# Column sums from strips: another form for the bias shifts, key sums and end terms of a four-layer network kernel

## The chip, the cores and the metric

The kernel runs on one core of a Trainium2 chip. The metric is the device time of one execution in microseconds (us). One launch computes the whole network for two images, one after the other on the same core.

## The reference

The input is two images of 512 channels and 64 x 64 pixels. Four layers follow each other, each in the form "x plus a branch of the group-normalised x" (32 groups of 16 channels):

```python
x = x + _L0_conv_ref(_gn(x), ...)   # window attention and pooled tokens
x = x + _L1_conv_ref(_gn(x), ...)   # deformable attention
x = x + _L2_conv_ref(_gn(x), ...)   # mixture of max pools
x = x + _L3_conv_ref(_gn(x), ...)   # random-feature ("favor") attention

def _gn(v, G=32, eps=1e-5):
    g = v.reshape(B_, G, C_ // G, H_, W_)
    m = jnp.mean(g, axis=(2, 3, 4), keepdims=True)
    s = jnp.var(g, axis=(2, 3, 4), keepdims=True)
    return ((g - m) / jnp.sqrt(s + eps)).reshape(v.shape)
```

The kernel never writes the normalised image. A projection `W.T @ (x - m) / s` is computed as `(W / s).T @ x` plus a bias per output channel, `(W / s).T @ (-m)`: a product of a 512 x 512 matrix with one vector, called the bias shift below. It is needed for W_sr, W_q and both halves of W_kv in layer 0, for w_q in layer 1, and for Wq, Wk and Wv in layer 3.

Layer 3 also needs sums over all 4096 tokens:

```python
qp = _favor_softmax_features(q, proj, is_query=True)
kp = _favor_softmax_features(k, proj, is_query=False)   # ratio * (exp(..) + EPS)
context = jnp.einsum('bhnm,bhnd->bhmd', kp, v)
k_sum = jnp.sum(kp, axis=-2)
denom = jnp.einsum('bhnm,bhm->bhn', qp, k_sum)
out = jnp.einsum('bhnm,bhmd->bhnd', qp, context) / denom[..., None]
```

`k_sum` is 256 feature sums for each of 8 heads. The constant EPS in the query's features makes two further terms, called end terms below: EPS times the sum of `context` over the 256 features (64 values a head), and EPS times the sum of `k_sum` (one value a head).

## The kernel before

An image lies in SBUF as X, 128 partitions by four chunks of channels (KC = 4) by 4096 pixels, in fp32. Y, of the same size, is scratch and later takes the next image. Work is done in blocks of 512 pixels (TB, one PSUM bank), eight blocks an image (NB). Almost all products run in fp32; in the profile each fp32 matmul shows as two MATMUL records with a LDWEIGHTS each.

The program is written down per engine as a chain of Python generators that are advanced in turn (`in_turn`), and a scheduler then fixes one order of instructions for each engine, adds the waits and hands out the buffers. An engine runs its instructions in that order, so an instruction that waits holds up all behind it on its engine.

The places that matter here, for each of the two images:

- **Layer 0, `pooled_tokens` (L1844).** W_sr is scaled by rows with 1/s on VectorE (`scale_rows`, L103), its bias shift is made (`shift_bias`, L108, called at L1851), and then 8 blocks of 4 projections run (`project`, L131, matmuls at L134), each read out by a Gelu on ScalarE (L1857) and two sums on VectorE. After blocks 1, 2 and 3 the weights of q, k and v are scaled and their shifts made (L1869).
- **Layer 1 (L984).** One shift, for `bq`. The next products (L1046) and the Gelu behind them need it.
- **Layer 3, `key_context` (L1365).** A shift for `bk` (L1375), and two rows: `v_row` (L1377), the shift of V as a row spread over all partitions, and `vmean` (L1410), the mean of V. Both come from `shift_row` (L122): four accumulating matmuls of 128x512 with the vector as the stationary operand, spread to 128 columns. Then keys and values of block n+1 are prepared (`prepare`) while block n is contracted (`contract`); POOL adds the exponentials of every head into `asum` (L1436). While the last block is contracted, the first query block is prepared: `Queries.first` makes the shift `bq3` (L1541).
- **Layer 3, `contexts` (L1456).** Once all keys are done: the largest score of each head (L1461 to L1472, `lost`), its product with the mean of V (`lv`, L1475), then for both halves j of the 256 features four transposes of the accumulated context (L1481) and sixteen one-column products that sum `asum` (L1489), and last thirty-two one-column products for the end terms (L1501). The queries' scores (L1693) follow on TensorE.

`shift_bias` is sixteen matmuls: for each of four output chunks, four accumulating products of a 128x128 block of the weights (stationary) with one column of `nmean` (moving). `contexts` uses the same form: a block of data is loaded as stationary operand and a single column of ones is moved through it. All of these write a few columns of one PSUM bank, which VectorE then reads (L118, L120, L1491, L1503).

All the pools of PSUM together hold 8 banks. In layer 0 the ring of working banks has 5, in layer 3's key part it has 8.

Of the kernel before, what the change touches and what calls it, by code (L numbers as in the profile page):

```python
# [33 lines left out]
    C_SD) = (0, 128, 256, 384, 512, 514, 540, 572, 573, 589, 717, 765, 797, 863)  # L34
C_N = 927
# [898 lines left out]
class Net(General):  # L934
# [14 lines left out]

    def local_bound(self, sp_scale, wp, pp):  # L950
# [14 lines left out]
    def layer1(self, X, Y, d):  # L965

        tc, nc, vec = self.tc, self.nc, self.vec
        with tc.tile_pool(name="l1", bufs=1) as sp:
# [5 lines left out]
            with tc.tile_pool(name="l1a", bufs=1) as wp, \  # L974
# [9 lines left out]
                self.shift_bias(bq, wq, nmean, pp)  # L984
# [380 lines left out]
    def key_context(self, X, Y, d, nmean, rstd, mv, queries, kp, wp, pp):  # L1365
# [9 lines left out]
        self.shift_bias(bk, wk, nmean, pp)  # L1375
        row = kp.tile([P, C], F32, name="v_row")
        self.shift_row(row, wv, nmean, pp)  # L1377
# [7 lines left out]
        def prepare(blk):  # L1385
# [70 lines left out]
    def contexts(self, top, acc, asum, vmean, queries, kp, pp):  # L1456
# [20 lines left out]
        yield  # L1477
        for j in range(2):
# [6 lines left out]
            ps = pp.tile([P, TB], F32, name="mm")  # L1485
            for h in range(NH):
                for i in range(2):
                    lo = i * NK + j * P
                    nc.tensor.matmul(ps[:, h:h + 1], asum[h][:, lo:lo + P], self.one[:, :1],  # L1489
                                     start=(i == 0), stop=(i == 1))  # L1490
            nc.vector.tensor_tensor(ksum[:, j, :], ps[:, :NH], lost, ALU.add)  # L1491
            yield
        ends = queries.ends
        ps = pp.tile([P, TB], F32, name="mm")
        for i in range(2):
            for g in range(NH):
                ch = slice(g % 2 * HD, (g % 2 + 1) * HD)
                for j in range(2):
                    src = ksum[:, j, g:g + 1].to_broadcast([P, HD]) if i else ctxm[:, j, g, :]
                    at = i * KC + g // 2  # L1500
                    nc.tensor.matmul(ps[ch, at:at + 1], src, self.one[:, :1], start=(j == 0),  # L1501
                                     stop=(j == 1))
        nc.vector.tensor_scalar(ends, ps[:, :2 * KC].rearrange("p (i c) -> p i c", i=2), 1e-4,  # L1503
                                None, ALU.mult)
# [19 lines left out]
class Queries:  # L1524
# [197 lines left out]
class Local:  # L1722
# [121 lines left out]
    def pooled_tokens(self):  # L1844
# [6 lines left out]
        net.shift_bias(bias, w, self.nmean, self.pp, self.vec[:, V_BSR:V_BSR + KC])  # L1851
        for blk in range(NB):
# [11 lines left out]
            if 1 <= blk <= 3:  # L1864
# [4 lines left out]
                net.shift_bias(self.bias["qkv"[i]], w3, self.nmean, self.pp,  # L1869
# [619 lines left out]
```

## Time and profile before

| | us |
|---|---|
| median of 3 runs | 5323.94 |
| lowest and highest of these | 5315.73, 5334.31 |
| the profiled execution's own time | 5318.67 |
| its span, first to last instruction | 5316.9 |
| TensorE busy in it | 4985.0 |
| VectorE, ScalarE, POOL busy | 3203.0, 1807.7, 1800.7 |
| mean granted TensorE clock | 0.965 |

The groups that the change touches, summed from the trace of this execution for both images: the one-column matmuls of `shift_bias` (L115) are 448 records, those of the key sums (L1489) 128, those of the end terms (L1501) 128; the matmuls of `shift_row` (L127) are 32.

How to read it: TensorE is busy for 94% of the span, but matmuls are pipelined and the record of one is longer than the time by which it delays the next. So the durations of single records are not added up below; the distance from the first record of a stretch to the start of what follows it is used. "Granted clock" is the share of the full TensorE clock that the chip's throttle allowed in a stretch.

### The profile page before, as it was taken

What the parts mean: (1) busy time and instruction counts of PE and PEld (TensorE: products, weight loads), DVE (VectorE), ACT (ScalarE), POOL (GpSimd) and SP (SyncE); (2) the same over time, 40 slices, a digit from 0 to 9 for tenths busy, and PEclk for the clock granted to TensorE, in tenths of its full rate; (3) what the DMA queues carried; (4) which work ended last, traced back from release to release, by engine and by line L of the source; (5) the groups of instructions that cost most, each with busy time, mean ns of one, the idle gap of its engine ahead of it and who ended that gap; (6) DMA issues with size and microseconds to landing.
All of it is one profiled execution on the core that took longest, in us unless ns stands there. A gap on an engine that the chain in (4) does not pass through costs nothing. (4 is left out here: it accounts for less than half of the span.)

```text
span 5316.9 us, 48977 instructions
## 1 busy us (share of the span) xinstructions
PE 4985.0 (94%) x17531; PEld 2129.3 (40%) x17531; DVE 3203.0 (60%) x3944; ACT 1807.7 (34%) x3441; POOL 1800.7 (34%) x1196
## 2 busy tenths in 40 slices
PE   7999999899988899999999999998999888999998
PEld 4423333554333344533344333335543334445333
DVE  4267777645679733477732677766456796333766
ACT  1245665234222233222112556652432122333221
POOL 0035565401310045444500355553013100454544
PEclk9999999999989999999999999999999899999999
DMA  3035556500000000211210355564000000000111
GB/s 145 2 79 139 145 141 172 151 18 24 1 1 0 1 1 1 64 43 52 73 55 2 91 141 143 141 176 135 18 24 1 1 0 1 1 1 17 40 46 43
DMA packets 124753, 309.89 MB, mean 58 GB/s; under 512 B 20882, under 2 KB 33682, under 8 KB 122964
## 3 DMA queue, kind: packets, MB, share of 16 engines
q1 hardware_dynamic: 124500, 306.67, 21.0%
q8 instruction: 141, 2.31, 0.2%
q14 instruction: 112, 0.92, 0.1%
HBM read 258.10 MB, written 48.50 MB: 58 GB/s over the span
## 5 line engine op out<-in xcount | busy, mean ns | idle before, releaser
L134 PE MATMUL mm<-big,w 128*128 128x512 f32 x2560 | 1191.2, 610 | 9.8 <-DVE late L2252 9.8
L134 PEld LDWEIGHTS mm<-big,w 128*128 128x128 f32 x2560 | 468.8, 192 | 693.6 <-issue 577.2
L2298 POOL TENSOR_TENSOR late<-late,big 128x1024 f32<-128x1024 f32 x192 | 454.1, 2365 | 204.0 <-DVE big L2293 188.5
L1266 POOL TENSOR_TENSOR total<-prob 128x512 f32<-128x512 f32 x128 | 159.6, 1269 | 758.6 <-ACT prob L1263 758.6
L1183 PE MATMUL acc<-big,dg 128*128 128x512 f32 x704 | 320.0, 613 | 55.6 <-DVE big L698 25.4
L1436 POOL TENSOR_TENSOR big<-big 128x512 f32<-128x512 f32 x224 | 277.5, 1270 | 222.8 <-ACT big L1427 222.8
L2220 POOL TENSOR_TENSOR late<-late 128x512 f32<-128x512 f32 x128 | 160.8, 1276 | 521.3 <-ACT late L2209 499.5
L2293 DVE TENSOR_TENSOR big<-big,mm 128x512 f32<-128x512 f32 x384 | 255.3, 681 | 122.8 <-ACT mm L2285 109.0
L698 DVE TENSOR_TENSOR big<-big 128x3968 f32<-128x3968 f32 x72 | 308.8, 4289 | 6.2
L2285 ACT COPY mm<-big 128x512 f32<-128x512 f32 x428 | 244.4, 593 | 196.0 <-DMA big<-rows 162.8
L1427 ACT ACTIVATE big<-mm,ed 128x256 f32<-128x256 f32 x512 | 193.8, 488 | 259.3 <-DVE top L1423 227.0
L1283 DVE RECIPROCAL recip<-psD 128x512 f32<-128x512 f32 x64 | 214.9, 3357 | 87.2 <-PE psD L1280 87.2
L2298 POOL TENSOR_TENSOR late<-late,tap 128x1024 f32<-128x1024 f32 x96 | 227.2, 2366 | 103.3 <-DVE tap L2293 100.1
L1263 ACT ACTIVATE prob<-mm 128x512 f32<-128x512 f32 x256 | 132.0, 605 | 364.4 <-PE mm L1260 359.2
L1423 DVE TENSOR_REDUCE top<-mm 128x1 f32<-128x512 f32 x256 | 159.1, 683 | 148.2 <-PE mm L1361 147.9
L1678 PE MATMUL mm<-k,w 128*128 128x512 f32 x512 | 236.3, 606 | 9.9 <-DVE k L1671 6.5
L2160 DVE TENSOR_TENSOR prod<-qs,big 128x1024 f32<-128x1024 f32 x192 | 230.3, 1215 | 8.3 <-PE tap L2173 6.3
L1401 PE MATMUL mm<-w,big 128*128 128x512 f32 x512 | 234.5, 601 | 0.0
L134 PE MATMUL mm<-big,big 128*128 128x512 f32 x512 | 232.6, 615 | 0.0
L1183 PEld LDWEIGHTS acc<-big,dg 128*128 128x128 f32 x704 | 136.3, 196 | 236.8 <-issue 193.5
L134 PE MATMUL mm<-big,wq 128*128 128x512 f32 x512 | 230.6, 599 | 0.0
L548 PE MATMUL mm<-big,wo 128*128 128x512 f32 x512 | 224.5, 596 | 0.0
(375 smaller groups left out, 8152.3 us busy)
## 6 DMA issues: line engine op xcount, KB each, us to landing
big<-rows SPq DMA_DIRECT2D x428, 256.0 KB, 4.3
tap<-rows SPq DMA_DIRECT2D x212, 256.0 KB, 4.3
yd<-late SPq DMA_DIRECT2D x32, 512.0 KB, 3.0
lost_all<-lost SPq DMA_DIRECT2D x128, 128.0 KB, 3.1
out<-big SPq DMA_DIRECT2D x64, 256.0 KB, 2.0
big<-in_W_kv SPq DMA_DIRECT2D x8, 1024.0 KB, 6.2
rows<-late SPq DMA_DIRECT2D x64, 128.0 KB, 2.4
big<-yd SPq DMA_DIRECT2D x16, 512.0 KB, 5.1
```

The source lines that it names most:

```text
L134: self.nc.tensor.matmul(ps, w[:, kc, :], X[:, kc, blk * TB:(blk + 1) * TB], start=(kc == 0), stop=(kc == KC - 1))
L548: nc.tensor.matmul(ps, w[:, kc, oc * P:(oc + 1) * P], att[:, kc, :], start=(kc == 0), stop=(kc == KC - 1))
L698: nc.vector.tensor_tensor(o, a, b, ALU.max)
L1183: nc.tensor.matmul(accs[b], dg, src[:, b * TB:(b + 1) * TB], start=(j == 0), stop=(j == 6))
L1283: nc.vector.reciprocal(r, psD)
L1401: nc.tensor.matmul(ps, X[:, kc, lo:lo + P], wv[:, kc, :], start=(kc == 0), stop=(kc == KC - 1))
L1436: nc.gpsimd.tensor_tensor(a, a, part, ALU.add)
L1678: nc.tensor.matmul(ps, self.wo[:, kc, oc * P:(oc + 1) * P], qs[:, kc, :], start=(kc == 0), stop=(kc == KC - 1))
L2160: self.nc.vector.tensor_tensor(self.prods[k % 3].rearrange("p (y x) -> p y x", x=W), qs, self.kx[:, y + dy:y + dy + self.UY, dx:dx + W], A ...
L2285: nc.scalar.copy(ps, part)
L2293: nc.vector.tensor_tensor(part.rearrange("p (y x) -> p y x", x=W), self.vx[:, y:y + self.UY // 2, dx:dx + W], ps.rearrange("p (y x) -> p y ...
L2298: nc.gpsimd.tensor_tensor(out, out, t, ALU.add)
```

## The change

Three pieces of arithmetic are written in another form; the sums are the same.

- `shift_bias` becomes `shift_columns`. Four matmuls of 32x512 (`shift_strips`) take one chunk of `nmean`, spread to 32 columns, as stationary operand and move the 512 weights of the chunk through it. Chunk kc writes partitions 32 kc to 32 kc + 31 of one bank. ScalarE copies the bank to a scratch tile in SBUF. Four matmuls then take 128 columns of that tile as stationary operand and one column of a constant (`C_ROW`, which has a one in one row of each strip) as moving operand, which adds the four strips and turns the row to a column. VectorE writes the result as before.
- `shift_row` becomes `shift_rows`: the strips, the copy, and then one matmul of 128x512 in place of the four accumulating ones.
- In `contexts` the key sums are made as strips: eight matmuls of 32x512 whose stationary operand is a constant of ones in every other column (`C_EVEN`), two for each of four strips. ScalarE copies one half of the bank, VectorE adds the other half, two transposes turn the strips to columns, and VectorE adds `lost`. The end terms come from VectorE's sums over `acc` and over the strips, with four one-column matmuls for the share of `lv` and one of four columns that spreads the heads' sums over the partitions.

One constant of four columns is added (`C_STRIP`), so the constants' load has 931 columns in place of 927. The scratch tile is a tile that is free at that time: one of layer 0's `sq` tiles, layer 1's `feats`, a further buffer of layer 3's `sq` ring.

```diff
+    def shift_strips(self, w, nmean, pp, scratch):
+        nc = self.nc
+        ps = pp.tile([P, TB], F32, name="mm")
+        for kc in range(KC):
+            nc.tensor.matmul(ps[32 * kc:32 * kc + 32, :], nmean[:, kc:kc + 1].to_broadcast([P, 32]),
+                             w[:, kc, :], start=True, stop=True)
+        nc.scalar.copy(scratch, ps)
+
+    def shift_columns(self, dst, w, nmean, pp, scratch, add=None):
+        nc = self.nc
+        self.shift_strips(w, nmean, pp, scratch)
+        ps = pp.tile([P, TB], F32, name="mm")
+        for oc in range(KC):
+            nc.tensor.matmul(ps[:, oc:oc + 1], scratch[:, oc * P:(oc + 1) * P],
+                             self.cst[:, C_ROW:C_ROW + 1], start=True, stop=True)
+        if add is None:
+            nc.vector.tensor_copy(dst, ps[:, :KC])
+        else:
+            nc.vector.tensor_tensor(dst, ps[:, :KC], add, ALU.add)
+
+    def shift_rows(self, dst, w, nmean, pp, scratch):
+        nc = self.nc
+        self.shift_strips(w, nmean, pp, scratch)
+        ps = pp.tile([P, TB], F32, name="mm")
+        nc.tensor.matmul(ps, self.cst[:, C_ROW:C_ROW + 1].to_broadcast([P, P]), scratch, start=True,
+                         stop=True)
+        nc.vector.tensor_copy(dst, ps)
...
-                self.shift_bias(bq, wq, nmean, pp)
+                self.shift_columns(bq, wq, nmean, pp, feats.rearrange("p k n -> p (k n)")[:, :TB])
...
-        self.shift_bias(bk, wk, nmean, pp)
+        scratch = lambda: wp.tile([P, TB], F32, name="sq", bufs=4)
+        self.shift_columns(bk, wk, nmean, pp, scratch())
         row = kp.tile([P, C], F32, name="v_row")
-        self.shift_row(row, wv, nmean, pp)
+        self.shift_rows(row, wv, nmean, pp, scratch())
...
-                self.shift_row(vmean, wv, gap, pp)
+                self.shift_rows(vmean, wv, gap, pp, scratch())
...
+        ends, heads = queries.ends, lambda a: a.rearrange("p (c h) -> p c h", h=2)
+        ps = pp.tile([P, TB], F32, name="mm")
+        for h in range(2):
+            for cc in range(KC):
+                nc.tensor.matmul(ps[32 * cc:32 * cc + 32, :], self.cst[:, C_EVEN + h:C_EVEN + h + 32],
+                                 asum[2 * cc + h], start=(h == 0), stop=(h == 1))
+        part = kp.tile([P, NK], F32, name="ksum_rows")
+        nc.scalar.copy(part, ps[:, :NK])
+        nc.vector.tensor_tensor(part, part, ps[:, NK:], ALU.add)
+        yield
+        ps = pp.tile([P, TB], F32, name="mm")
+        for j in range(2):
+            nc.tensor.transpose(ps[:, j * P:(j + 1) * P], part[:, j * P:(j + 1) * P], self.ident)
+        nc.vector.tensor_tensor(
+            ksum.rearrange("p j (c h) -> p j c h", h=2),
+            ps[:, :NK].rearrange("p (j c r) -> p j c r", j=2, r=32)[:, :, :, :2],
+            bcast(heads(lost), 1, 2), ALU.add)
         for j in range(2):
...
-            ps = pp.tile([P, TB], F32, name="mm")
-            for h in range(NH):
-                for i in range(2):
-                    lo = i * NK + j * P
-                    nc.tensor.matmul(ps[:, h:h + 1], asum[h][:, lo:lo + P], self.one[:, :1],
-                                     start=(i == 0), stop=(i == 1))
-            nc.vector.tensor_tensor(ksum[:, j, :], ps[:, :NH], lost, ALU.add)
-            yield
-        ends = queries.ends
-        ps = pp.tile([P, TB], F32, name="mm")
-        for i in range(2):
-            for g in range(NH):
-                ch = slice(g % 2 * HD, (g % 2 + 1) * HD)
-                for j in range(2):
-                    src = ksum[:, j, g:g + 1].to_broadcast([P, HD]) if i else ctxm[:, j, g, :]
-                    at = i * KC + g // 2
-                    nc.tensor.matmul(ps[ch, at:at + 1], src, self.one[:, :1], start=(j == 0),
-                                     stop=(j == 1))
-        nc.vector.tensor_scalar(ends, ps[:, :2 * KC].rearrange("p (i c) -> p i c", i=2), 1e-4,
-                                None, ALU.mult)
+            yield
+        total, own = (kp.tile([P, n], F32, name=f"ends_{n}") for n in (1, KC))
+        nc.vector.tensor_reduce(total, part, AX.X, ALU.add)
+        nc.vector.tensor_scalar(own, self.cst[:, C_STRIP:C_STRIP + KC], total, None, ALU.mult)
+        nc.vector.tensor_reduce(ends[:, 0], acc, AX.X, ALU.add)
+        ps = pp.tile([P, TB], F32, name="mm")
+        for cc in range(KC):
+            nc.tensor.matmul(ps[:, cc:cc + 1], lv[:, 2 * cc:2 * cc + 2].rearrange("p h c -> p (h c)"),
+                             self.mean[:, :1], start=True, stop=True)
+        nc.tensor.matmul(ps[:, KC:2 * KC], self.cst[:, C_ROW:C_ROW + P], own, start=True, stop=True)
+        nc.vector.scalar_tensor_tensor(ends[:, 0], ps[:, :KC], 1.0 * NK * C / P, ends[:, 0],
+                                       ALU.mult, ALU.add)
+        for h in range(2):
+            ch = slice(h * HD, (h + 1) * HD)
+            nc.vector.scalar_tensor_tensor(ends[ch, 1], heads(lost)[ch, :, h], 1.0 * NK,
+                                           ps[ch, KC:2 * KC], ALU.mult, ALU.add)
+        nc.vector.tensor_scalar(ends, ends, 1e-4, None, ALU.mult)
         yield
...
-        self.net.shift_bias(self.bq, self.wq, nmean, pp)
+        self.net.shift_columns(self.bq, self.wq, nmean, pp,
+                               self.wp.tile([P, TB], F32, name="sq", bufs=4))
...
-        net.shift_bias(bias, w, self.nmean, self.pp, self.vec[:, V_BSR:V_BSR + KC])
+        net.shift_columns(bias, w, self.nmean, self.pp, self.sq[3],
+                          self.vec[:, V_BSR:V_BSR + KC])
...
-                net.shift_bias(self.bias["qkv"[i]], w3, self.nmean, self.pp,
-                               self.vec[:, at:at + KC])
+                net.shift_columns(self.bias["qkv"[i]], w3, self.nmean, self.pp, self.sq[i],
+                                  self.vec[:, at:at + KC])
...
+    cst[:, C_STRIP:C_STRIP + KC] = p[:, None] // 32 == np.arange(KC)
```

More of the change, by code (lines that the diff above doesn't have):

```diff
@@ L33 @@
 (C_ID, C_GRP, C_MEAN, C_ONE, C_E2, C_TAP, C_Y, C_X, C_MH, C_ROW, C_TAPW, C_E32, C_EVEN,
-    C_SD) = (0, 128, 256, 384, 512, 514, 540, 572, 573, 589, 717, 765, 797, 863)
-C_N = 927
+    C_SD, C_STRIP) = (0, 128, 256, 384, 512, 514, 540, 572, 573, 589, 717, 765, 797, 863, 927)
+C_N = 931
 V_BQ, V_BK, V_BSR, V_LNG, V_LNB, V_QE, V_TEMP = 0, 4, 12, 16, 20, 24, 28
```

## The prediction

> **What bounds the kernel now.** I read the busy table first, then the timeline around every place that the diff touches, then windows of the granted clock, and last the timeline of a place that already works with strips.
>
> ```profile
> PE 4985.0 (94%) x17531; PEld 2129.3 (40%) x17531; DVE 3203.0 (60%) x3944; ACT 1807.7 (34%) x3441; POOL 1800.7 (34%) x1196
> ```
>
> TensorE sets the time, so what counts is the time by which a place delays the next matmul. In layer 0 (timeline; columns: start, us, engine, line, operation):
>
> ```profile
> 69.86 3.63 PE L115 MATMUL mm<-gn_nmean,big 128*128 128x1 f32 x32
> 73.35 2.82 PE L134 MATMUL mm<-big,big 128*128 128x512 f32 x6
> ```
>
> One shift is 32 records (16 fp32 matmuls of two passes) and holds TensorE from 69.86 to 73.35: 3.49 us, 0.11 a pass. ScalarE and VectorE wait for TensorE there, so this is on the path.
>
> At the end of layer 3's keys:
>
> ```profile
> 2229.34 3.78 PE L1489 MATMUL mm<-cst,big 128*128 128x1 f32 x32
> 2232.98 1.31 PE L1481 MATMUL mm<-cst,ctx_acc 128*128 128x128 f32 x5
> 2234.08 6.83 PE L1489 MATMUL mm<-cst,big 128*128 128x1 f32 x32
> 2240.84 1.89 PE L1501 MATMUL mm<-cst,ctxm 128*64 128x1 f32 x32
> 2242.56 1.87 PE L1501 MATMUL mm<-cst,ksum 128*64 128x1 f32 x32
> 2244.79 3.78 PE L1693 MATMUL mm<-k,proj 64*128 64x512 f32 x8 [0.36 <-DVE ksum_ratio L1556]
> 2246.87 1.08 ACT L1696 ACTIVATE qf<-mm 128x512 f32<-128x512 f32 x2 [17.41 <-PE mm L1693]
> ```
>
> 128 one-column passes stand between the keys and the queries; ScalarE sits idle for 17.41 us. The second group of 32 takes 6.83 us where the first took 3.78, and the eight score passes take 3.78 where the same eight take 1.99 at 2252.73. The reason is in the windows (last figures: granted clock, DMA share, GB/s):
>
> ```profile
> 2226.00:2236.00 10.00, 9.92 (x68) 8.54 (x67) 5.14 (x10) 2.07 (x7) 4.72 (x4) 0.83 0.65 212
> 2236.00:2248.00 12.00, 11.64 (x96) 9.60 (x95) 4.47 (x11) 1.08 (x2) 0.00 (x0) 0.50 0.42 133
> 2248.00:2270.00 22.00, 21.55 (x59) 8.24 (x57) 21.08 (x30) 9.86 (x18) 8.73 (x7) 0.96 0.00 1
> ```
>
> "Busy" TensorE ran at half clock. The strips have a precedent in the key loop:
>
> ```profile
> 1854.41 1.07 PE L1339 MATMUL mm<-sq,e2h 128*32 128x512 f32 x8
> 1855.40 3.70 PE L1401 MATMUL mm<-w,big 128*128 128x512 f32 x8
> 1855.62 0.58 ACT L1341 COPY sq<-mm 128x512 f32<-128x512 f32 x1 [3.85 <-PE mm L1339]
> ```
>
> Eight passes of 32x512 hold TensorE for 0.99 us, eight of 128x512 for some 3.5 (0.43 a pass). The four strips run side by side. The copy starts 1.21 us after the first strip.
>
> [...]
>
> **The change, part by part.** From the built program's order of instructions: only the touched places move; POOL's order is the same, and SP's differs in the size of one load. In every place the second half (columns) stands directly behind the strips on TensorE, so TensorE waits there for ScalarE's copy with all its later work queued behind. The new wait at full clock: strips at 0, copy at 1.21, its end at 1.79, next weights 0.06 later (the gap that L2077 shows behind its copy, 206.34 to 206.40): columns start at 1.85. Four fp32 columns are 8 passes, 0.11 each, with a first weight load that nothing hides (0.19): 1.1 us. A shift is then 2.95 us in place of 3.49.
>
> (1) Layer 0, b_q, b_k, b_v, six shifts: -0.5 each. The Gelu in ScalarE's queue ahead of the copy (70.06 to 70.75) ends before the strips do, so it costs nothing. For the first image that is -1.5. In the second image the old shifts also brought half clock: a window 2710.70 to 2714.00 reads 0.51 and 2727.90 to 2734.60 reads 0.51; at half clock 3.4 and 6.8 us lose 1.7 and 3.4. With under 2 us of thin work a shift, I expect less of this; [...]I count half: 2.5. Image two: -4.
>
> (2) Layer 0, b_sr, at half clock: 33.11 to 41.63 before, one full matmul slipped in between. After: the fourth chunk is scaled about 34.2, strips 1.7 (twice 0.86), copy 0.8, columns 8 x 0.21 = 1.7, next projection about 38.5. The slipped matmul (0.86) comes back. -2.2 and, in image two with two slipped, -1.7.
>
> (3) Layer 1, bq, half clock: the stretch 1079.47 to 1088.06; after, by the same steps, about 1084.9, and two L1046 matmuls that were inside it return (4 passes of 0.45): -1.4 each. The Gelu's table load (1.28 us at 1088.80) then follows earlier, and ends before its first matmuls do.
>
> (4) Layer 3, bk and v_row, half clock: 1823.68 to 1837.15 before. After: scaling of the fourth chunk 1824.9, strips to 1826.7, copy to 1827.5, columns to 1829.2, strips to 1831, copy to 1831.9, one full matmul of 1.7 to 1833.6: 3.5 us earlier. But the clock rose at about 1837 after the dense L127 matmuls; they go, and the projections behind have to warm it up themselves. That gives back about 2.3 (half of the full-rate work that L127 did while warming): -1.2 each[...].
>
> (5) Layer 3, v_mean: 2185.82 to 2189.35 was 3.5; now 1.85 + 0.86 + 0.2: -0.5. bq3: 2193.86 to 2197.52 was 3.66; now its strips are split around three L1441 matmuls, 0.95 + 1.0 and the same wait, then columns; the scores (L1361) start about 2198.6 with all eight to go where before one was done and the rest started at 2199.69: -1.1, and the window behind it, which also loses clock, -0.5. -2.1 each.
>
> (6) `contexts`: L1468 ends about 2229.0. First strip quartet to 2230.0. In the second, the last strip waits for POOL's last sum (L1436, 2225.78 + 4.94 = 2230.72) and ends at 2231.7: a wait that was hidden, and is now late next. ScalarE copies 256 columns: not shown in this form; between nothing and the 0.58 of 512, I take 0.35, from 2231.9. VectorE adds 256 columns (0.42, as L1447): 2232.7. Two and eight transposes at 0.165 (L1345, 0.66 for four) to 2234.4, four lv columns (8 passes) to 2235.3, one more matmul to 2235.7 (L1468, 0.38), three small VectorE operations of 0.17, scores at 2236.3. Before: 2244.79. That is -8.5. VectorE's new 128x1024 sum (twice L1423's 0.62) runs before `lost`, which waited for POOL until 2230.7 anyway (L1473, 1.27 us for eight columns), so nothing. Then the clock: if it stays full, the scores and the projection behind gain 1.8 + 0.6 more[...]. I take -9, between -7 and -11. DMA doesn't bind: `asum` is free earlier, so the next image's load moves with it.
>
> Sum: image one 2.2 + 1.5 + 1.4 + 1.2 + 2.1 + 9 = 17.4; image two 1.7 + 4 + 1.4 + 1.2 + 2.1 + 9 = 19.4. Together 37 us on the profiled execution's 5318.67: 5282. The median of the runs is 5.3 above that execution, so 5287.
>
> **The rivals.** *The copy and the clock take half back:* [...]part (6) gives 7, the small shifts nothing: 2 x (7 + 2) = 18, 5306. For it: [...]four places are at half clock already. Against: thin work falls from 128 passes to 10 in part (6).
>
> *Hidden:* another engine is late next, so less than 5 us remain, 5320. Against: ScalarE waits 17.41 us and VectorE for TensorE at all these places.
>
> *Slower:* the strips run one after another, because their moving operands are four different weight chunks. A quartet is then 3.43 at full clock, 6.9 at half. A shift would be 5.2 for 3.49 (8 places, +1.7), at half clock +2.5 (6 places); rows +1.7 and +2.7, two each; `contexts` still -4.3 twice. Sum +28: 5352. It decides once a quartet costs over about 2.2 us in place of 1.0 (22 quartets, a third of them at half clock, against 37). Against: L1339 moves four different `sq` tiles and takes 0.99.
>
> **How the numbers follow.** Forecast 0.69, half back 0.16, hidden 0.05, slower 0.10. The forecast's own bounds: part (6) from -7 to -11 and part (4) from 0 to -6 for each image[...], so 5270 to 5300; to leave out no more than 2 in 10 the range reaches past the half-back case: 5268 to 5311. About 0.3% (16 us) is what a measurement of this kernel can tell: faster takes the forecast and half of the half-back case (0.76), same the other half and the hidden case with some drift (0.13), slower 0.11.
>
> **What would show it.** Right: quartets of about 1 us, copies that start 1.2 us behind them, the distance from L1468's form to the first scores near 8 us in place of 16, and a clock near full between there and 12 us later. Wrong: quartets over 2 us; ScalarE's copy late behind a Gelu or an exponential; half clock remaining at the scores; the time to the first scores unchanged because they wait for VectorE.

## The result, and the profile after

The changed kernel takes 5278.93 us (median of 4 runs, 5270.48 to 5283.06), the kernel before 5326.10 in the same session (4 runs, 5315.73 to 5334.31): a ratio of 0.991, with an interval from 0.989 to 0.993. The forecast was 5287, with a range from 5268 to 5311. The profiled execution took 5283.06, with a span of 5281.3. It is the longest of its four, while the profiled execution before (5318.67, span 5316.9) was among the shortest of its kernel, so the two spans differ by 35.6 and the medians by 47.

The busy table after:

```profile
PE 4925.9 (93%) x17115; PEld 2044.1 (39%) x17115; DVE 3205.4 (61%) x3956; ACT 1817.7 (34%) x3461; POOL 1800.6 (34%) x1196
```

TensorE is busy 59 us less. The other engines are where they were, but for the new copies and sums: 10 us more on ScalarE and 2 on VectorE.

A shift in layer 0 (timeline after; the place of L115 before):

```profile
65.51 1.06 PE L955 MATMUL mm<-big,gn_nmean 128*32 128x512 f32 x8
65.61 0.69 ACT L1905 ACTIVATE late<-mm,b_sr 128x512 f32<-128x512 f32 x1 [2.75 <-PE mm L134]
66.64 0.58 ACT L957 COPY sq<-mm 128x512 f32<-128x512 f32 x1 [0.34 <-PE mm L955]
67.28 1.05 PE L965 MATMUL mm<-cst,sq 128*128 128x1 f32 x8 [0.71 <-ACT sq L957]
68.19 10.12 PE L134 MATMUL mm<-big,big 128*128 128x512 f32 x23
```

The quartet (the four strip products, eight records at L955) holds TensorE for about 1 us. The copy starts 1.13 behind the first strip and the columns 1.77, of which TensorE idles 0.71; the next projection starts 2.68 behind the first strip. The Gelu at 65.61 ends before the strips do, as the prediction had it.

The end of layer 3's keys (timeline after; POOL's last four sums, from 2220.05 for 4.97 us, end at 2225.02). A word on line numbers: the prediction's "L1468" is the small matmul that spreads the largest score of each head, behind which the key sums begin. In the changed kernel it is L1500, and L1468 is POOL's sum.

```profile
2223.22 2.90 PE L1514 MATMUL mm<-big,cst 128*32 128x512 f32 x16
2226.16 0.37 ACT L1517 COPY ksum_rows<-mm 128x256 f32<-128x256 f32 x1 [2.44 <-PE mm L1514]
2226.56 0.42 DVE L1518 TENSOR_TENSOR ksum_rows<-ksum_rows,mm 128x256 f32<-128x256 f32 x1 [0.79 <-ACT ksum_rows L1517]
2227.04 0.44 PE L1522 MATMUL mm<-cst,ksum_rows 128*128 128x128 f32 x2 [0.92 <-DVE ksum_rows L1518]
2227.31 1.04 PE L1530 MATMUL mm<-cst,ctx_acc 128*128 128x128 f32 x8
2228.19 0.95 PE L1541 MATMUL mm<-cst,lost_v 128*128 128x1 f32 x8
2229.00 0.36 PE L1543 MATMUL mm<-ends,cst 128*128 128x4 f32 x2
2229.94 1.99 PE L1740 MATMUL mm<-k,proj 64*128 64x512 f32 x8 [0.58 <-DVE ends L1548]
```

From the copy to the scores every engine waits for the one before it in turn, and all of it takes 3.8 us. The eight score passes take 1.99, where they took 3.78. The windows of the clock after (columns: stretch, its length, busy time of TensorE, weight loads, VectorE, ScalarE and POOL, granted clock, DMA share, GB/s):

```profile
2212.00:2222.00 10.00, 9.44 (x53) 4.73 (x51) 3.19 (x6) 4.02 (x10) 5.91 (x6) 1.00 0.18 53
2222.00:2230.00 8.00, 6.50 (x46) 3.53 (x46) 6.00 (x17) 0.71 (x3) 3.02 (x3) 1.00 0.88 263
2230.00:2242.00 12.00, 12.00 (x36) 4.75 (x38) 12.00 (x19) 5.50 (x10) 6.73 (x6) 1.00 0.36 132
```

TensorE was busy 81% of the middle stretch, before 97% of the stretch from 2236 to 2248; yet now the clock is full (1.00, before 0.50). VectorE, busy for all 12 us of the last line, comes up again below.

Where the time went, in the stretches around the touched places (us from the start of the first to the start of the second, image 1 / image 2). "Again" is a second series of the changed kernel, experiment 3:

| stretch | before | after | again |
|---|---|---|---|
| layer 0: statistics to the block behind b_q | 42.73 / 43.56 | 37.40 / 40.88 | 40.08 / 39.50 |
| layer 0: the two blocks with b_k and b_v | 34.61 / 39.65 | 33.21 / 33.21 | 33.21 / 33.21 |
| layer 1: statistics to the first queries | 24.07 / 24.06 | 22.70 / 22.70 | 21.77 / 21.77 |
| layer 3: statistics to the first projection | 15.87 / 15.89 | 11.24 / 11.03 | 11.24 / 12.72 |
| layer 3: v_mean to the scores behind it (L127 to L1361 / L955 to L1392) | 3.53 / 3.53 | 2.88 / 2.88 | 2.88 / 2.88 |
| layer 3: these scores to the largest-score matmul, with bq3 (to L1468 / L1500) | 39.29 / 39.29 | 37.14 / 37.14 | 37.15 / 37.15 |
| layer 3: from there to the first scores | 16.15 / 16.15 | 7.03 / 7.03 | 7.03 / 7.02 |
| layer 3: first scores to the next query block | 24.49 / 24.50 | 22.10 / 22.10 | 22.10 / 22.10 |
| sum | 407.37 | 350.67 | 351.81 |

The places gained 56.7 us in one profile and 55.6 in the other; the spans fell by 35.6 and, in the second series, 46.7 (5270.2). The rest of the program gave 21 and 9 back. Of this, about 5 is there in both, behind the first query block of image 1 (397.03 before, 402.36 and 401.69 after); of the rest, the larger part in the first profile (7.1 and 4.7) lies in layer 0's body, behind the shifts, which the change doesn't touch. One long stretch of it in image 1 (L2173 / L2221 to layer 1's statistics) took 810.19 before, and 816.04 and 809.98 in the two profiles of one and the same kernel.

### The profile page after: what moved, and what is told of

It is laid out like the page before. It is cut to its first block, busy times and chain, and to the rows that moved or that the text cites. A ratio compares the mean times of both kernels' runs of the same rounds, so it can differ in the third digit from the quotient of the medians.

```text
span 5281.3 us, 48171 instructions
## 1 busy us (share of the span) xinstructions
PE 4925.9 (93%) x17115; PEld 2044.1 (39%) x17115; DVE 3205.4 (61%) x3956; ACT 1817.7 (34%) x3461; POOL 1800.6 (34%) x1196
## 3 DMA queue, kind: packets, MB, share of 16 engines
q1 hardware_dynamic: 124500, 306.67, 20.7%
## 5 line engine op out<-in xcount | busy, mean ns | idle before, releaser
L1468 POOL TENSOR_TENSOR big<-big 128x512 f32<-128x512 f32 x224 | 277.6, 1270 | 219.5 <-ACT big L1459 219.5
```

The source lines that it names most:

```text
L1468: nc.gpsimd.tensor_tensor(a, a, part, ALU.add)
```

## The experiments

The theory was that two things act together: the shorter work itself (fewer passes, one wait for a copy), and the clock, which read half behind one-column passes (0.50 from 2233 to 2249 in the kernel before). A rival was that the clock has no part and the passes alone count; another, of the prediction, that strips would run one after another. The first four share one set of runs of the kernel before (median 5326.40), the next four another (5325.20), and the last has its own (5328.71); across these sets the ratios are compared. Experiments 1, 2 and 5 to 9 are edits of the changed kernel, 4 of the kernel before.

**1. The end of the keys alone**, all shifts in the old form:

```diff
 def shift_columns(self, dst, w, nmean, pp, scratch, add=None):
-    self.shift_strips(w, nmean, pp, scratch)
...
-    for oc in range(KC):
-        nc.tensor.matmul(ps[:, oc:oc + 1], scratch[:, oc * P:(oc + 1) * P],
-                         self.cst[:, C_ROW:C_ROW + 1], start=True, stop=True)
...
+    for oc in range(oc_n):
+        for kc in range(KC):
+            nc.tensor.matmul(ps[:, oc:oc + 1], w[:, kc, oc * P:(oc + 1) * P],
+                             nmean[:, kc:kc + 1], start=(kc == 0), stop=(kc == KC - 1))
...
 def shift_rows(self, dst, w, nmean, pp, scratch):
-    self.shift_strips(w, nmean, pp, scratch)
...
+    for kc in range(KC):
+        nc.tensor.matmul(ps, nmean[:, kc:kc + 1].to_broadcast([P, P]), w[:, kc, :],
+                         start=(kc == 0), stop=(kc == KC - 1))
...
```

> The changed kernel with the bias shifts and rows back in their old form (sixteen one-column matmuls a shift, four accumulating matmuls a row); key sums and end terms stay in the new form. Theory (each place saves what its own stretch shows): the stretch from L1468's matmul to the first scores stays near 7.0 us in place of 16.15, so two images give 18 us, and 2 to 4 us more behind it for the clock: 18 to 22 us below the kernel before. Rival (most of the gain is the shifts, whose half clock spread over their neighbourhood): under 12 us. Rival (the gain is the throttle's luck in other stretches): anything from +5 to -35, with the stretch itself as in the changed kernel.

Measured: 5307.61, ratio 0.9964 (0.9952 to 0.9976), 18.8 us, as expected. From L1468's form to the scores it takes 7.02 in both images. The old shifts now brought half clock in image 1 (0.51 from 73.8 to 80.7, 0.50 from 94.3 to 101.1), where they had not before (the three shifts of b_q, b_k and b_v took 3.49 us each, at 1.00): the two blocks with b_k and b_v took 41.69 in place of 34.61, with the same instructions. So what an old shift costs hangs on where half clock falls.

**2. The shifts alone**, `contexts` in the old form:

```diff
...
         for j in range(2):
...
+            ps = pp.tile([P, TB], F32, name="mm")
+            for h in range(NH):
+                for i in range(2):
+                    lo = i * NK + j * P
+                    nc.tensor.matmul(ps[:, h:h + 1], asum[h][:, lo:lo + P], self.one[:, :1],
+                                     start=(i == 0), stop=(i == 1))
...
```

> The changed kernel with the key sums and end terms back in the old form; shifts and rows stay in the new form. Theory: the remainder of the 47 us, some 25 to 30 us below the kernel before: in the traces of both kernels the stretches around the shifts differ by 4.5, 2.2, 3.8, 0.7 and 2.1 us in the first image and by 1.9, 7.2, 4.1, 0.7 and 2.1 in the second (29 us), and the two halves add up to the whole within 6 us. Rival (contexts hold nearly all): under 15 us.

Measured: 5285.88, ratio 0.9925 (0.9913 to 0.9938), 40.5 us, 10 more than expected. The gain of 1 and that of 2 make 59 together; the whole change makes 52 in the same session (experiment 3). Each of these medians is uncertain by some 6 us, so the parts add up as far as that can be told. The shifts, which the prediction had at about half of the gain, are the larger part.

**3. The changed kernel once more**, as it is, for the comparison with the others and for a second profile.

> The changed kernel unchanged, for a second profile and a closer interval. Theory: 40 to 52 us below the kernel before. In the first profile the stretch of layer 0 between the last shift and layer 1 was 7.1 us longer than before in the first image and 4.7 in the second, with nothing changed in it; [...]it differs by several us in this profile, and the places where half clock stands move. Rival (the change itself slows that stretch, by a buffer or an order): it is 5 to 7 us longer again in both images.

Measured: 5274.15, ratio 0.9901 (0.9887 to 0.9916), 52.2 us. This is the measure for all that follows. Its profile is the column "again" above. The stretch of layer 0 that the expectation names took 968.8 / 972.6 us before, 975.9 / 977.2 in the first profile and 966.9 / 976.4 here: 9 us less in image 1, 0.8 less in image 2. So the two profiles show scatter in image 1 alone; in image 2 other edits of the same kernel brought 967.8 (experiment 7) to 976.8 (5 and 8), which speaks against a fixed loss there too.

**4. The kernel before with 64 columns in place of one**, in all shifts that make columns and in the key sums; as many passes and the same reads, each result merely 64 times. The end terms kept one column.

```diff
-                nc.tensor.matmul(ps[:, oc:oc + 1], w[:, kc, oc * P:(oc + 1) * P],
-                                 nmean[:, kc:kc + 1], start=(kc == 0), stop=(kc == KC - 1))
+                nc.tensor.matmul(ps[:, 64 * oc:64 * oc + 64], w[:, kc, oc * P:(oc + 1) * P],
+                                 nmean[:, kc:kc + 1].to_broadcast([P, 64]), start=(kc == 0),
+                                 stop=(kc == KC - 1))
...
-                    nc.tensor.matmul(ps[:, h:h + 1], asum[h][:, lo:lo + P], self.one[:, :1],
-                                     start=(i == 0), stop=(i == 1))
+                    nc.tensor.matmul(ps[:, 64 * h:64 * h + 64], asum[h][:, lo:lo + P],
+                                     self.one[:, :64], start=(i == 0), stop=(i == 1))
...
```

> The kernel before with the one moving column of the shifts and of the key sums repeated to 64 columns (the same number of matmuls, every 64th column is read; end terms and rows as before). It separates the clock from the number of products. Theory[...]: passes stay at 0.11, the granted clock stays full through the key sums (16.15 us become about 12.5) and at the shifts of the second image, so 12 to 22 us below the kernel before. Rival (the number of products is what counts, the half clock is a sign of waiting elsewhere): within 5 us of the kernel before, and 0.5 remains in the windows at the key sums. Rival (a wider moving operand costs more): some 448 + 128 passes longer by up to half, so 20 us above.

Measured: 5295.68, ratio 0.9944 (0.9932 to 0.9956), 30.7 us, more than the 12 to 22 expected. The end of the keys in its timeline:

```profile
2230.71 3.68 PE L1491 MATMUL mm<-cst,big 128*128 128x64 f32 x32
2234.32 1.12 PE L1504 MATMUL mm<-cst,ctxm 128*64 128x1 f32 x32
2235.28 1.10 PE L1504 MATMUL mm<-cst,ksum 128*64 128x1 f32 x32
2236.73 3.35 PE L1696 MATMUL mm<-k,proj 64*128 64x512 f32 x8 [0.36 <-DVE ksum_ratio L1559]
```

and the window around it:

```profile
2227.00:2236.00 9.00, 9.00 (x125) 8.93 (x124) 4.29 (x8) 0.00 (x0) 1.07 (x1) 1.00 0.80 263
```

Thirty-two passes of 64 columns take 3.68, as many as thirty-two of one took at full clock (3.78), and the second group no longer takes 6.83. The end terms, still of one column, take 1.1 where they took 1.9. The clock is full throughout; only the scores, behind the one-column end terms, are slow once more (3.35). At b_k and b_v of image 1, where the clock had been full with the old shift too, nothing changed (17.31 a block, as before). So the filled columns themselves gain nothing but the clock: 16.15 to 10.74 from L1468's form to the scores, 5.4 of the 9.1 that the change gains there. Over the touched stretches it is 25.9 of 55.6, in the medians 31 of 52. About half of the change's gain can be had by the clock alone; the rival that has the clock play no part falls.

At layer 1's bq, though, where the clock was half already when the shift began, the 64 columns didn't bring it back (the same run):

```profile
1080.10:1083.50 3.40, 3.40 (x17) 3.23 (x15) 0.05 (x1) 0.00 (x0) 0.00 (x0) 0.50 0.77 312
1083.50:1086.90 3.40, 3.40 (x18) 3.40 (x17) 0.00 (x0) 0.00 (x0) 0.00 (x0) 0.50 0.02 5
1086.90:1090.30 3.40, 3.40 (x9) 2.42 (x9) 0.45 (x2) 1.69 (x2) 0.00 (x0) 0.50 0.00 0
1090.30:1093.70 3.40, 3.40 (x9) 1.57 (x8) 0.00 (x0) 0.35 (x2) 0.00 (x0) 0.99 0.00 0
```

The shift ends at 1086.8, and the clock is full only behind 3.4 us of dense products. Layer 1's stretch stayed at 23.95 and 24.08 (24.07 before).

**5. Strips one after another.** All four products accumulate in the same 32 partitions, which is to put them one behind the other; columns and rows are made from 32 partitions. `contexts` keeps its strips.

```diff
-            nc.tensor.matmul(ps[32 * kc:32 * kc + 32, :], nmean[:, kc:kc + 1].to_broadcast([P, 32]),
-                             w[:, kc, :], start=True, stop=True)
-        nc.scalar.copy(scratch, ps)
+            nc.tensor.matmul(ps[:32, :], nmean[:, kc:kc + 1].to_broadcast([P, 32]),
+                             w[:, kc, :], start=(kc == 0), stop=(kc == KC - 1))
+        nc.scalar.copy(scratch[:32], ps[:32])
...
```

> The changed kernel with the four strips of a shift written one on top of the other: the four matmuls accumulate into partitions 0 to 31, so they can't run side by side; copy, columns and row take 32 partitions in place of 128, and the sums are the same. Key sums keep their four strips. Theory (strips run side by side, and that is what makes a shift short): a quartet takes 3.4 us in place of 1.0 at full clock, so ten places cost 2.4 us each and eight at half clock about 3 each[...]: 45 to 50 us above the changed kernel, about as slow as the kernel before, within 12 us of it. Rival (most of the gain of the shifts is that the thin products are gone, whatever replaces them): less than 20 us above the changed kernel.

Measured: 5306.91, ratio 0.9966 (0.9954 to 0.9978), 18.3 us better than before and, by the ratios, about 34 worse than with strips side by side: less than the 45 to 50 expected, more than the rival's 20. A shift in its timeline:

```profile
67.73 3.62 PE L955 MATMUL mm<-big,gn_nmean 128*32 128x512 f32 x8
72.01 1.05 PE L965 MATMUL mm<-cst,sq 32*128 32x1 f32 x8 [0.67 <-ACT sq L957]
72.99 7.56 PE L134 MATMUL mm<-big,big 128*128 128x512 f32 x17
```

The quartet takes 3.62 and the whole shift 5.26, as the slower rival had worked it out (5.2). A block with b_k takes 19.19 for 17.31, near what it had worked out (+1.7). But at the places that were at half clock the rival expected 2.5 more a shift, and there layer 1's stretch is 24.20 and 24.48 (24.07 before) and layer 3's start 14.98 and 15.85 (15.87). The passes are longer, but half clock lasted only 6.8 us at bq of image 1, where it lasted 17.1 before and 13.7 with the strips side by side. What the shifts gain in the changed kernel thus needs the strips side by side: with serial ones the time is that of experiment 1, which has no new shifts at all (5307.61).

**6. Columns later.** For b_q, b_k and b_v the strips stay, but the columns are made one output chunk into the next block, so that TensorE has eight dense passes to do while ScalarE copies.

```diff
...
             for oc in range(KC):
+                if oc == 1 and 2 <= blk <= 4:
+                    i = blk - 2
+                    at = (V_BQ, V_BK, V_BK + KC)[i]
+                    net.shift_columns(self.bias["qkv"[i]], self.fold[:, i], self.nmean, self.pp,
+                                      self.sq[i], self.vec[:, at:at + KC], strips=False)
...
-                net.shift_columns(self.bias["qkv"[i]], w3, self.nmean, self.pp, self.sq[i],
-                                  self.vec[:, at:at + KC])
+                net.shift_strips(w3, self.nmean, self.pp, self.sq[i])
```

> The changed kernel with the columns of b_q, b_k and b_v set one projection group later on TensorE than their strips, so that ScalarE's copy lies beside a projection (six places, two images). Theory: the wait for the copy, 0.7 us from the end of the strips to the first column, goes six times: the stretches from block to block fall from 16.6 to about 15.8, 4 to 5 us below the changed kernel in all. Rival (the wait is hidden by the pipeline or the drain of the strips): no change in these stretches.

Measured: 5268.44, ratio 0.9900 (0.9885 to 0.9915). In its timeline:

```profile
65.36 1.06 PE L955 MATMUL mm<-big,gn_nmean 128*32 128x512 f32 x8
66.36 3.70 PE L134 MATMUL mm<-big,big 128*128 128x512 f32 x8
69.89 0.95 PE L966 MATMUL mm<-cst,sq 128*128 128x1 f32 x8
```

The wait is gone: 15.82 a block in place of 16.59, in all four places that can be compared. That is 0.8 each and would be 4.6 over six shifts. The ratios can't tell it from experiment 3 (0.9900 and 0.9901).

**7. Work for TensorE in the pauses of the statistics.** Before every scaling of weights the group means pass through two small products, and TensorE idles around them (3.67, 1.04 and 2.12 us at bq in the first profile after). Here it runs matmuls whose result nobody reads.

```diff
+        self.fill(pp, [X[:, KC - 1, b * TB:(b + 1) * TB] for b in (NB - 2, NB - 1)])
         ps = pp.tile([P, TB], F32, name="mm")
         nc.tensor.matmul(ps[:, :KC], self.grp, mv[:, :, 0], start=True, stop=True)
...
+        self.fill(pp, [nmean[:, :1].to_broadcast([P, NK])])
...
+        self.fill(pp, [var[:, :1].to_broadcast([P, TB])] * 2)
...
+    def fill(self, pp, moving):
+        for a in moving:
+            ps = pp.tile([P, TB], F32, name="mm")
+            self.nc.tensor.matmul(ps[:, :a.shape[1]], self.grp, a, start=True, stop=True)
```

> The changed kernel with five matmuls more in each group statistics (three layers, two images) whose results nobody reads: two of 128x512 that wait for the last blocks of the image, one of 128x256 behind the means, two of 128x512 behind the variances. They fill TensorE's waits of 1 to 4 us ahead of the shifts of b_sr, bq and bk. Theory (the clock is halved by the idle windows ahead of these shifts, and the shifts and what follows pay for it): half clock there shrinks from 10 to 14 us a place to 3 or less, the stretches from the statistics to the first full blocks fall by 2 to 4 us a place, 10 to 20 us below the changed kernel. Rival (fillers only lengthen the chain of the statistics, which sets the time): 3 to 8 us above it.

Measured: 5264.06, ratio 0.9885 (0.9870 to 0.9900). Layer 1's bq in experiment 3's windows (same columns as above):

```profile
1072.00:1078.00 6.00, 3.74 (x15) 1.47 (x15) 1.67 (x4) 0.59 (x1) 0.92 (x1) 0.63 0.87 351
1078.00:1084.00 6.00, 6.00 (x16) 3.70 (x17) 0.45 (x2) 1.85 (x2) 0.00 (x0) 0.72 0.00 0
```

and in experiment 7's:

```profile
1072.00:1078.00 6.00, 5.35 (x20) 2.32 (x19) 2.76 (x11) 0.17 (x1) 1.02 (x1) 1.00 0.74 267
1078.00:1084.00 6.00, 5.33 (x21) 2.71 (x19) 0.45 (x2) 1.87 (x2) 0.00 (x0) 1.00 0.32 126
```

The clock is full, and the stretch falls to 20.68 in both images (21.77 in experiment 3, 24.07 before), layer 3's start to 9.80 and 10.18, layer 0's to 36.42 and 36.43. These six stretches, counted from the second small product, are 12.9 us shorter than in experiment 3; but the fillers ahead of that product put it about 2 us later in all. By the ratios the kernel is 8.5 us faster than in experiment 3, though the two intervals overlap. At bq, the half clock that the strips had left (0.63 and 0.72 in these stretches) thus goes once the pause ahead of them is filled (1.00 in both).

**8. The next image's statistics later.** Behind the first queries of image 1, TensorE in experiment 3's timeline waits for VectorE:

```profile
2244.60 0.27 PE L1664 MATMUL mm<-cst,sq_cols 128*64 128x128 f32 x1
2248.72 0.63 PE L1664 MATMUL mm<-cst,top_col 128*64 128x128 f32 x2 [3.85 <-DVE top_col L1660]
2249.28 3.68 PE L1707 MATMUL psO<-qf,ctxm 128*64 128x512 f32 x8
```

In the kernel before, the same wait was 1.94:

```profile
2271.49 0.41 PE L1617 MATMUL mm<-cst,top_col 128*64 128x128 f32 x2 [1.94 <-DVE top_col L1613]
2271.82 1.94 PE L1660 MATMUL psO<-qf,ctxm 128*64 128x512 f32 x8
```

In experiment 3 VectorE is busy from 2224 to 2248 without a pause, partly with the statistics of the image that comes next. Here these are put behind the residual sums of the block before:

```diff
         for b in range(NB):
-            self.nc.vector.bn_stats(st[:, kc, b, :], X[:, kc, b * TB:(b + 1) * TB])
+            with self.net.tc.issue_after(self.done):
+                self.nc.vector.bn_stats(st[:, kc, b, :], X[:, kc, b * TB:(b + 1) * TB])
...
-            nc.vector.tensor_tensor(xx, xx, ps, ALU.add)
+            self.done = nc.vector.tensor_tensor(xx, xx, ps, ALU.add).ins
```

> The changed kernel with VectorE's statistics of the next image (32 operations of 0.6 us in the first image) held back until the block of queries beside which they are written has come, in place of the first score stage. In all three profiles with the new key sums, the first image's stretch from the first query block's scores to the end of layer 3 took 402 us, in the kernels with the old ones 397. Theory (with the scores 9 us earlier, VectorE's statistics are late next: TensorE waits for the maxima of the scores behind them): that stretch falls by 3 to 6 us in the first image, nothing changes in the second, 3 to 6 us below the changed kernel. Rival[...]: the stretch stays at 400 to 403, or the gain is lost in the later blocks.

Measured: 5265.03, ratio 0.9887 (0.9872 to 0.9902). The place in its timeline:

```profile
2242.74 0.27 PE L1665 MATMUL mm<-cst,sq_cols 128*64 128x128 f32 x1
2242.85 0.38 PE L1665 MATMUL mm<-cst,top_col 128*64 128x128 f32 x2
2243.16 1.94 PE L1708 MATMUL psO<-qf,ctxm 128*64 128x512 f32 x8
```

The wait of 3.85 is gone, and the products behind it take 1.94 for 3.68: in experiment 3 the clock was half from 2247.3 to 2254.1, here it is full from 2240 to 2248. The first output projection starts 42.6 us behind the first scores, where it was 47.2 in both profiles of the changed kernel and 46.8 before. From these transposes (L1664, in the kernel before L1617) to those of the next block it took 38.8 us before, 43.2 in both profiles of the changed kernel and 37.2 here, as in image 2 of the changed kernel (37.2 and 37.4), which has no image behind it. In the six profiles with the new key sums and without this edit it is 43.1 to 43.6, in the three with the old ones 38.8 or 38.9. Once held back, the statistics take part of it back: behind the last block's transposes the layer needs 45.1 us for 43.5. The gain in this block is shown; the ratio as a whole again can't be told from experiment 3's.

**9. The three together** (6, 7 and 8).

> The changed kernel with the columns one projection group later, the fillers in the group statistics and VectorE's statistics of the next image held back, all three. Theory (they work in different stretches and add up): 4.6 + about 9 + 4 us, so 15 to 19 us below the changed kernel, near 5257 us, 66 to 70 below the kernel before. Rival ([...]layer 0's long stretch scatters by 7 us): 8 to 12 us below the changed kernel.

Measured: 5254.49 (5250.84 to 5258.51), ratio 0.9863 (0.9846 to 0.9879): 74 us below the kernel before, a little more than the 66 to 70 expected, and an interval that doesn't meet experiment 3's. It is faster than both kernels. Layer 0's start takes 34.74 in both images, its blocks 15.82, layer 1's start 20.7, layer 3's 10.2.

## Why the prediction was right

The mechanism and the sign were right, and the time lay within the range, 8 us under the forecast in the first series and 13 in the second. That it lay so near is in part luck: the places gave half as much again as predicted, and what was given back elsewhere was not in the sum. By its steps, for both images (predicted; measured in the two profiles of the changed kernel):

| step | predicted | after | again |
|---|---|---|---|
| (1) and (2), layer 0 | -9.4 | -15.9 | -14.6 |
| (3) layer 1, bq | -2.8 | -2.7 | -4.6 |
| (4) layer 3, bk and v_row | -2.4 | -9.5 | -7.8 |
| (5) v_mean and bq3 | -4.2 | -5.6 | -5.6 |
| (6) `contexts` and the clock behind it | -18 | -23.0 | -23.0 |
| given back elsewhere | 0 | +21 | +9 |

**The wait for the copy** was worked out at 1.85 to the columns and 2.95 for a shift; it measured 1.77 and 2.68. So at full clock a shift gains 0.8 where 0.5 was counted. Experiment 6 shows that the wait is there and is worth the 0.8 that the sum gave it.

**(1) and (2): the term of the clock was too small.** The prediction counted half of the 5.1 us that image 2 lost at half clock, as an estimate. All of it came back: the two blocks of image 2 fell from 39.65 to 33.21, the same as image 1's. Experiment 1 shows that image 1 could have had this loss as well, and more. (2) gave about 4.6 and 2.0 in the first profile, 1.9 and 3.4 in the second, for 2.2 and 1.7. For b_sr the prediction has half clock in both images; the granted clock is listed as 0.50 in image 2 (2670 to 2679), but as 1.00 in image 1 (33.1 to 41.6), although its records there have the same 352 ns, against 250 at the full clock of b_q.

**(3)** is right at its place; the two profiles differ by 0.9 an image.

**(4): "that gives back about 2.3" did not come true.** The prediction let the projections pay for half clock, since the dense L127 matmuls, behind which the clock had risen (from 0.50 to 1.00 at 1836.7), were gone. The windows before, around this place:

```profile
1821.00:1828.00 7.00, 4.68 (x22) 4.64 (x23) 3.74 (x11) 0.00 (x0) 1.01 (x1) 0.65 0.08 20
1828.00:1837.00 9.00, 9.00 (x21) 5.29 (x22) 0.16 (x1) 0.00 (x0) 0.00 (x0) 0.52 0.00 0
```

and after:

```profile
1821.00:1828.00 7.00, 3.99 (x12) 1.32 (x11) 4.41 (x18) 0.17 (x1) 1.01 (x1) 0.52 0.07 20
1824.60:1828.00 3.40, 3.26 (x8) 0.73 (x8) 3.00 (x9) 0.00 (x0) 0.00 (x0) 0.50 0.00 0
1828.00:1831.40 3.40, 2.05 (x16) 1.12 (x16) 0.16 (x1) 1.14 (x2) 0.00 (x0) 0.99 0.00 0
1831.50:1834.80 3.30, 3.30 (x4) 1.50 (x5) 0.69 (x1) 0.00 (x0) 0.00 (x0) 0.50 0.00 0
```

and the two quartets in the timeline after:

```profile
1824.72 3.26 PE L955 MATMUL mm<-w,gn_nmean 128*32 128x512 f32 x8 [2.05 <-issue]
1829.64 1.06 PE L955 MATMUL mm<-w,gn_nmean 128*32 128x512 f32 x8
```

Before, half clock lasts from 1823.1 to 1836.7; after, the clock is full as soon as 1828, directly behind the first quartet and before any dense product, and later half for 3.4 us only, from 1831.5. The first quartet took 3.26, more than the 1.8 of the prediction, and still paid: the second took 1.06. The prediction expected it behind dense products alone, but here full clock came behind 3.40 us of which a quartet filled 3.26. In image 1 of the second profile the same happened, while in its image 2 the quartet filled only 2.39 of the 3.4 us from 4438.6, the clock stayed half until 4452.3, and the gain was 3.2. No run isolates what the clock goes by here. The other gains were 4.6 and 4.9: within the bounds that the prediction had set from 0 to -6, but near their far end.

**(5)** came out a third larger: v_mean gave 0.65 for 0.5, the stretch with bq3 2.15 for 1.6. Experiment 4 gets nearly all of the latter (39.29 to 37.24) without a single pass less, so most of it can be had by the clock here too, where the prediction gave 1.1 of the 1.6 to the shorter work.

**(6)** The path was right step by step. POOL's last sum is late next, as predicted: TensorE waits for it inside the second quartet, and from the copy to the scores it takes 3.8 where 4.4 were worked out. L1468's form to the scores fell by 9.1 (predicted 8.5). The clock stayed full, so the 2.4 that the prediction named for this case came on top (24.49 to 22.10); it had then hedged the two, by estimate, to -9 an image, between -7 and -11, and the runs give -11.5, just outside. Ten transposes and ten thin passes went by at 1.00 here (2222 to 2230), but in the company of the quartets, so no run tells what transposes alone would do.

**What it did not have:** the 4.7 to 5.3 us behind the first queries of image 1. The prediction asked of every vanished stall what is late next, and found POOL; one block further on it is VectorE, since the next image's statistics fill it there. In image 2, which has no image behind it, the same stretch is 1.4 and 1.0 us shorter than before. Experiment 8 removes the wait, and shows that the loss is there: the block behind it, 4.4 us longer than before, becomes 6.0 shorter, and the whole stretch is back to 397.73. In experiment 9, where the wait is gone too, the stretch is 401.22: the block takes 39.5 (its clock is 0.83, in experiment 8 0.86), and the end of the layer, behind the last block's transposes, 46.0 for 43.5. With the held-back statistics alone that end takes 45.1, with the fillers alone 45.3; how the two share in it isn't settled.

**The rivals.** "Half back" and "hidden" are refuted by the medians. The slower rival's price of a serial shift was right at full clock (5.2; its own terms, 2.95 and the quartet's 2.44 more, make 5.4; measured 5.26), and its two premises were wrong: the strips do run side by side with four different weight chunks (1.06 for the eight passes, 3.62 one behind the other), and serial ones would not have cost 2.5 more at the places of half clock. Serial strips in `contexts` weren't tried; serial shifts give 5307, not its 5352.

All told, 37 predicted, 56 to 57 found at the places, 9 to 21 given back. About 5 of what was given back belongs to the change. Most of the rest in the first profile lies in layer 0's body, where two profiles of one kernel differ by 9 us in image 1; so it is put down to the scatter of single executions, over which the medians (47 and 52) average.

## What to carry to other kernels

Where thin products stand on TensorE's path, price the clock apart from the passes and look at the stretch behind them as well: of the 9.1 us gained at the key sums the clock alone was 5.4 (experiment 4), and the scores and the projection behind them gained 2.4 more. Strips of 32 partitions that run side by side were cheap here (1.06 us for eight passes of 512 columns, 3.62 one behind the other), and among dense products the clock stayed full behind them (1.00 from 2222 to 2242); the copy that they need cost about 0.7 us of TensorE's time, which other dense work can cover (experiment 6: 0.8 a place). Where the clock is half before the thin work begins, look at the pause ahead of it (experiment 7: layer 1's stretch from 21.77 to 20.68). When a stall of 9 us goes, follow the path past the place for a block or two, because an engine that had slack there may now be the one that is late.

## What the runs showed of the hardware

A busy TensorE is not one that keeps its clock. Passes of one column, back to back at 0.11 us, were followed by half clock. In the kernel before, at the first key sums (same columns as above):

```profile
2229.30:2232.70 3.40, 3.40 (x33) 3.40 (x32) 1.96 (x2) 0.16 (x1) 1.42 (x2) 1.00 0.82 253
2232.70:2236.10 3.40, 3.40 (x19) 3.40 (x18) 1.55 (x3) 0.00 (x0) 0.00 (x0) 0.50 0.71 257
```

Passes of 64 columns at the same 0.11 us left it full (1.00 from 2227 to 2236 in experiment 4, which gained 31 us of 5326). But where it was half already, at bq, two stretches of 3.4 us nearly full of such passes, now at 0.21 us each, did not raise it (0.50 until 1090.3). So the time in which TensorE is busy doesn't tell the clock: by the records it was busy for all 3.40 us ahead of the halving, and for all of the 9 us in which 64 columns left the clock full. No run isolates where the limit lies.

Behind quartets of 32-row strips both were seen. One that filled 3.26 of the 3.40 us up to 1828 was followed by full clock. The 3.4 us behind it, with columns, a short quartet and waits for copies (TensorE busy 2.05 of 3.40 us), were followed by half clock from 1831.5; and at bq of the first profile, where TensorE was busy for 2.73 of the 3.40 us from 1080.5, nearly all of it with the quartet, half clock went on until 1090.8. In serial form (experiment 5) layer 1's stretch was at most 0.4 us longer than before, although the eight passes take 3.62 in place of 1.06 at full clock.

Where half clock falls moves things that nobody touched. In the traces of both kernels each stretch of half clock lasts a multiple of 3.4 us (3.4 at the least and 30.7 at the most before, 17.1 at the key sums; 13.7 at bq after), as does the one at 94.3 in experiment 1 (6.8); where these stretches begin differs from program to program. The old shifts of image 1 took 34.61 in one program and 41.69 in another, and a stretch of 810 us differed by 6 between two profiles of the same program. Only the sums over places that were touched, or medians, may be compared at this size.
